# Products of zeros in the planned gaps of TensorE, in a two-layer adaLN and FFN kernel

## The chip, the cores and the metric

The kernel runs on one core of a Trainium2 chip. The metric is the device time of one execution in microseconds (us), the median of several. The engines are named as in the profile: PE (TensorE, matrix products; its weight loads are shown as PEld), DVE (VectorE), ACT (ScalarE), POOL (GpSimd) and SP (SyncE, which issues most of the DMAs).

## The reference: what is computed

`x` is 128x32x256 (batch, time, features), `cond` is 128x256. Two residual layers follow each other:

```python
# layer 0: an ODE with RK4, 32 time steps, driven by x[:, t, :], from q0 = p0 = cond
i_couple = jnp.tanh(q) @ coupling.T
dq = q - q ** 3 / 3.0 - p + drive + i_couple + bias
dp = EPSILON * (q + ALPHA - BETA * p)
...
# its trace of q goes through a gated FFN whose operands are block-quantised (blocks of 32)
inter = jax.nn.silu(_mx_linear(q, w_gate)) * _mx_linear(q, w_up)
x = x + _mx_linear(inter, w_down)
# layer 1: modulated RMS norm, attention over the 32 time steps with 16 heads of 16,
# q and k RMS-normed per head; then a gated FFN with Hadamard rotation, 8-bit activations
# and ternary weights
xn = _rms_norm(x, g_norm) * (1.0 + scale) + shift
q, k, v = split(xn @ W_qkv)
o = softmax(q @ k.T * d ** -0.5) @ v
o = o + o @ W_out
x = x + h_bitlinear(silu(h_bitlinear(o, w_gate)) * h_bitlinear(o, w_up), w_down)
```

## The kernel before

The batch of 128 fills the partitions. **Phase one** runs 32 time steps. Each step has four RK4 stages (`step`, `slope`): a PSUM slot is opened by a product of zeros (`opened`, L458), DVE adds a linear combination into it (`nest`, L513), PE adds scaled copies of the drive and of earlier stages (`plus`, L548) and the product with the coupling matrix (L562), ACT makes tanh and square (L555, L556), POOL the cube (L569). L606 makes the new state. The FFN of layer 0 for that time step (`ffn0`) follows: a transpose on PE (L487), block maxima and scales on DVE (L649, L627, L632, L639), a multiplication (L861), clipping (L841), scaling on POOL (L867, L909, L917), a DMA transpose (L395), gate and up products (L882) with silu and multiplication (L890, L894), the down product (L929). The result is stored, RMS-normed (ACT L941, POOL L946 and L947, ACT L951), multiplied and shifted on POOL (L955, L959), transposed on PE (L487) and copied to `xnT` by ACT (L964). The weights are quantised on the way: those of layer 0 in the first 90 us, mostly on DVE, the ternary ones of layer 1 near the end of the phase (PE L730, DVE L736, L740, L741, L746, L751).

**Phase two** works through 32 tiles of 128 tokens (`tokens`): q, k and v (L1043, L1050), a power on POOL for the norms (L1063, L1064), multiplication and 32x32 transposes on DVE (L1069, L1076, L1088, L1090), logits in 32x32 tiles of PE (L1098), softmax (L1113, L1117, L1120, L1121), attention times v, also in 32x32 tiles (L1128), the output rotation (L487, L1146, L1151), 8-bit quantisation (L1018, L1025, L1026, L1167, L1171), a DMA transpose, gate and up (L1184, ACT L1192, DVE L1199), a Hadamard transform (L1215 on DVE and POOL, L487, L1221, L1226), quantisation again (L1234, L1238), a DMA transpose and the down product (L1249, L1256).

**The order.** No engine takes its instructions in the order of the source. Every piece of work is an `Item` with an engine, a cost in us and the buffers that it reads and writes, and `Work` plans them. `Work.run` simulates all engines with these costs, forwards and backwards; `Work.order` repeats that up to 30 times, keeps the plan that ends first, and gives each buffer (`Buf`) its place (`Slot`). The items are then emitted in the order of their planned start, first those of phase one (rank under 100), then those of phase two, with other PSUM tiles in between. Each engine runs its instructions in that order and waits on semaphores for what it needs. The planned times are a model's: on the chip the gaps of an engine lie elsewhere or aren't there.

**PSUM slots.** A slot is a region of a PSUM bank. Slots that matter here: `ps_stage` (the RK4 stages), `ps_turn` (two halves of one bank, for transposes), `ps_gu` (two banks, gate and up of layer 0), `ps_po` (down product of layer 0); in phase two `ps_one` (four banks) and `ps_two` (two tiles of 1024 columns). A buffer takes a slot when its first writer starts, and the slot is free again when its last reader is done.

Of the kernel before, what the change touches and what calls it, by code (L numbers as in the profile page):

```python
# [20 lines left out]
P = 128  # L21
# [17 lines left out]
PE, DVE, ACT, POOL, SP = "PE", "DVE", "ACT", "POOL", "SP"  # L39
# [30 lines left out]
class Buf:  # L70


    def __init__(self, slots):
        self.slots, self.slot = slots, None
        self.writers, self.readers, self.left = [], [], 0
        self.end, self.fixed, self.pool = 0.0, False, None
# [11 lines left out]
class Item:  # L88


    def __init__(self, engine, cost, fn, rank, table, port, tail, records):
        self.engine, self.cost, self.fn, self.rank = engine, cost, fn, rank
        self.table, self.port, self.tail, self.records = table, port, tail, records
        self.after, self.before, self.open = [], [], 0
        self.bufs, self.outs, self.small, self.behind = [], (), False, ()
        self.ready, self.start, self.end = 0.0, None, None


class Work:
# [7 lines left out]
    LOAD, COLD = 1.3, 0.1  # L107
    BLOCK, FETCH = 128, 3.2
    ROUNDS = 30

    def __init__(self):
        self.items = []
# [143 lines left out]
    def order(self):  # L256

        for item in self.items:
            for a in item.after:
                a.before.append(item)  # L260
            for b in item.bufs:
                b.fixed = b.slot is not None
            item.prio = item.rank
        best = math.inf
        for n in range(self.ROUNDS):
            self.strict = n > 0
            done = self.run(True)
            end = max(item.end for item in done)
            if end < best:
                best, chosen = end, done  # L270
                places = [(b, b.slot) for item in done for b in item.bufs]
            for item in self.items:
                item.prio = -item.end
            self.strict = True
            self.run(False)
            for item in self.items:
                item.prio = -item.end
        for b, slot in places:
            b.slot = slot
        return chosen  # L280


@with_exitstack
def kernel(
# [22 lines left out]
    nc = tc.nc  # L307
    B, T, N = x.shape
# [12 lines left out]
    def tile_of(name, shape, dtype=F32):  # L321
        return const.tile(shape, dtype, name=name)
# [59 lines left out]
    work = Work()  # L382
# [69 lines left out]
    zeros = tile_of("zeros", [P, N], BF16)  # L452
# [536 lines left out]


    KPADS, VPADS = 3, 4
    PHASE_TWO = 100.0

    k_pads, v_pads = [], []
    pads_ready = []
# [35 lines left out]
    def tokens(g):  # L1031
        rank = PHASE_TWO + g
        tok = slice(g * P, (g + 1) * P)
# [228 lines left out]
        tokens(g)  # L1262

    issue = work.order()
    with tc.manual_schedule():
        for item in issue:
            if item.rank < PHASE_TWO:
                item.fn()
    phase_one.close()
    ps_2 = ctx.enter_context(tc.tile_pool(name="ps_2", bufs=1, space=PSUM))  # L1270
    for i, slot in enumerate(ps_one):
        slot.ap = ps_2.tile([P, HALF], F32, name=f"ps_one{i}")
    for i, slot in enumerate(ps_two):
        slot.ap = ps_2.tile([P, FF], F32, name=f"ps_two{i}")
    with tc.manual_schedule():
        for item in issue:
            if item.rank >= PHASE_TWO:
                item.fn()


# [50 lines left out]
```

## Time and profile before

| what | value |
|---|---|
| median of 3 runs | 874.21 us (872.87 to 882.12) |
| profiled execution | 884.23 us, its span 882.5 us |
| mean granted clock of PE | 0.956 |
| PE busy | 781.6 us (89%), 10300 products |
| PE weight loads | 590.1 us (67%) |
| DVE busy | 749.4 us (85%), 1885 instructions |
| ACT busy | 499.3 us (57%) |
| POOL busy | 636.4 us (72%) |

The span runs from the first instruction's start to the last one's end. A product's record on PE is longer than the time that it keeps the next one waiting: products are pipelined and their ends are modelled, so that "busy" holds the latency of the last one in each run. A matrix product of f32 operands appears as two records. The clock row gives the share of full speed that PE was granted. In a timeline a row is start, duration, engine, line, operation, output and inputs, shape, count, and in brackets the idle time of the engine before it, with the instruction that ended it. Phase one ends near 428 us, phase two begins with L1043 at 429.58.

### The profile page before, as it was taken

Reading aid. Unit: us, or ns where it says so; the run is one execution under the profiler, and the core shown is the slowest. Engines: PE = TensorE matmul, PEld = TensorE weight load, DVE = VectorE, ACT = ScalarE, POOL = GpSimd, SP = SyncE. Lnnn points to the kernel's source line nnn. Section 1 sums busy time; section 2 is a strip of 40 time slices with the busy share of each in tenths; the row PEclk is TensorE's granted clock in tenths of the full one; section 3 lists DMA queues with packets and bytes.
Section 4 is the critical chain, followed back from the end, with each engine's and each line's share of the span. In section 5 each row is a group of like instructions: output and inputs, shape, how many; then the busy total and the mean of one; then the engine's idle time right before and its main releaser. Section 6 shows DMA issues by size and latency. Waiting matters only on the chain. (4 is left out here: it accounts for less than half of the span.)

```text
span 882.5 us, 25579 instructions
## 1 busy us (share of the span) xinstructions
PE 781.6 (89%) x10300; PEld 590.1 (67%) x10300; DVE 749.4 (85%) x1885; ACT 499.3 (57%) x1014; POOL 636.4 (72%) x619
## 2 busy tenths in 40 slices
PE   7788999999999999994678989998999988988974
PEld 4566777778887887872344666866677665766654
DVE  5989999899999999998157978997989769798882
ACT  4243455555665665654324666767677647576653
POOL 5645898878899988799699649658866477766330
PEclk9989999999999999997769999999999989999997
DMA  8211332222322442425200122222122212122132
GB/s 265 66 32 42 71 77 57 71 57 67 70 73 73 106 99 65 105 65 99 47 2 15 24 45 48 64 56 56 19 56 56 55 36 56 37 54 44 47 70 66
DMA packets 128887, 55.49 MB, mean 63 GB/s; under 512 B 102144, under 2 KB 127616, under 8 KB 128768
## 3 DMA queue, kind: packets, MB, share of 16 engines
q1 hardware_dynamic: 128768, 53.85, 26.2%
q8 instruction: 81, 1.33, 0.6%
q14 instruction: 38, 0.31, 0.1%
HBM read 21.32 MB, written 8.39 MB: 34 GB/s over the span
## 5 line engine op out<-in xcount | busy, mean ns | idle before, releaser
L1064 POOL TENSOR_TENSOR tiny<-tiny,neg_half 128x32 f32<-128x32 f32 x32 | 175.1, 5472 | 2.7
L1215 POOL TENSOR_TENSOR wide<-wide 128x512 f32<-128x512 f32 x64 | 82.1, 1300 | 99.7 <-DVE wide L1215 60.8
L562 PEld LDWEIGHTS ps_stage<-slim,coup 128*128 128x128 f32 x1024 | 132.2, 194 | 14.3 <-ACT slim L555 5.2
L562 PE MATMUL ps_stage<-slim,coup 128*128 128x128 f32 x1024 | 138.9, 279 | 0.1
L569 POOL TENSOR_TENSOR slim<-slim,slim 128x256 f32<-128x256 f32 x96 | 73.6, 767 | 37.3 <-ACT slim L556 35.5
L1215 DVE TENSOR_TENSOR wide<-wide 128x512 f32<-128x512 f32 x128 | 87.9, 715 | 0.3
L548 PE MATMUL ps_stage<-drives,eye 128*128 128x256 f32 x256 | 81.2, 400 | 5.3 <-DVE ps_stage L513 3.8
L548 PE MATMUL ps_stage<-slim,eye 128*128 128x256 f32 x256 | 78.0, 394 | 7.6 <-DVE slim L513 7.6
L555 ACT ACTIVATE slim<-slim 128x256 f32<-128x256 f32 x96 | 39.5, 411 | 70.9 <-DVE slim L513 58.3
L1043 PE MATMUL ps_one<-w_qkv_sb,xnT 128*128 128x512 f32 x128 | 69.4, 671 | 2.1 <-DVE coup L1076 0.9
L917 POOL TENSOR_TENSOR wide_bf<-mid,tiny 128x512 bf16<-128x512 fp8e4 x64 | 67.7, 1064 | 3.9 <-DVE mid L841 3.7
L909 POOL TENSOR_TENSOR mid<-mid,tiny 128x512 f32<-128x512 f32 x64 | 66.3, 1049 | 4.1 <-DVE tiny L639 3.7
L1226 PE MATMUL ps_two<-had_ffn,wide 128*128 128x128 f32 x512 | 64.6, 282 | 4.3 <-DVE tiny L1025 1.6
L1226 PEld LDWEIGHTS ps_two<-had_ffn,wide 128*128 128x128 f32 x512 | 61.8, 196 | 8.4 <-DVE tiny L1025 2.1
L548 PEld LDWEIGHTS ps_stage<-slim,eye 128*128 128x128 f32 x256 | 43.5, 193 | 24.1 <-DVE slim L513 15.2
L1128 PEld LDWEIGHTS ps_one<-v_pad,mid 32*32 32x32 f32 x4096 | 42.2, 107 | 25.1 <-issue 15.5
L1199 DVE SCALAR_TENSOR_TENSOR wide<-ps_two,tiny,mid 128x512 f32<-128x512 f32 x64 | 46.5, 737 | 13.1 <-ACT mid L1192 12.9
L1128 PE MATMUL ps_one<-v_pad,mid 32*32 32x17 f32 x4096 | 47.8, 182 | 10.4 <-issue 5.9
L1192 ACT ACTIVATE mid<-ps_two,tiny 128x512 f32<-128x512 f32 x64 | 42.9, 686 | 21.9 <-PE ps_two L1184 21.0
L556 ACT ACTIVATE slim<-slim 128x256 f32<-128x256 f32 x96 | 38.9, 406 | 26.0 <-DVE slim L513 25.8
L1234 ACT ACTIVATE wide<-ps_two,magic,tiny 128x1024 f32<-128x1024 f32 x32 | 38.5, 1202 | 24.6 <-DVE tiny L1026 18.3
L548 PEld LDWEIGHTS ps_stage<-drives,eye 128*128 128x128 f32 x256 | 40.4, 195 | 14.3 <-DVE ps_stage L513 9.0
(153 smaller groups left out, 2065.7 us busy)
## 6 DMA issues: line engine op xcount, KB each, us to landing
x_step<-in_x_dram SPq DMA_DIRECT2D x32, 128.0 KB, 2.3
x_add<-in_x_dram SPq DMA_DIRECT2D x32, 128.0 KB, 2.1
x_dram<-slim SPq DMA_DIRECT2D x32, 128.0 KB, 1.7
slim<-x_dram SPq DMA_DIRECT2D x32, 128.0 KB, 2.2
out_dram<-slim SPq DMA_DIRECT2D x32, 128.0 KB, 1.7
raws<-in_L_ffn_w_gate_dram SPq DMA_DIRECT2D x4, 512.0 KB, 5.0
raws<-in_L_ffn_w_up_dram SPq DMA_DIRECT2D x4, 512.0 KB, 5.6
raws<-in_L_ffn_w_down_dram SPq DMA_DIRECT2D x4, 512.0 KB, 3.6
```

Of the source, the lines that this page charges most:

```text
L548: PE, cost, lambda: nc.tensor.matmul(ps[i].ap, lhsT=eyes[eye], rhs=src.ap, start=False, stop=False),
L562: nc.tensor.matmul(ps[i].ap[:, sl], lhsT=coup[i][:, c, sl], rhs=two(th.ap)[:, c, :], start=False, stop=(c == NC - 1 and m == NC - 1),)
L569: POOL, 0.685, lambda: nc.gpsimd.tensor_tensor(sq.ap, sq.ap, qi.ap, MULT),
L909: lambda it=it, ks=ks: nc.gpsimd.tensor_tensor(blocks(it.ap), blocks(it.ap), spread(binv.ap[:, ks], BLOCK), MULT),
L917: lambda b8=b8, ks=ks, sl=sl: nc.gpsimd.tensor_tensor(blocks(bq.ap[:, sl]), blocks(b8.ap), spread(bscl.ap[:, ks], BLOCK), MULT),
L1043: nc.tensor.matmul(pqk.ap, lhsT=xnT_flat[:, c, tok], rhs=w_qkv_sb[:, c, : 2 * N], start=(c == 0), stop=(c == NC - 1),)
L1064: nc.gpsimd.tensor_tensor(rstd.ap, rstd.ap, neg_half, ALU.pow)
L1128: nc.tensor.matmul(by_v(po.ap)[row, hd, :], lhsT=by_head(exT.ap)[row, hd, :], rhs=v_pad.ap[row, hd, :], start=True, stop=True,)
L1192: lambda pgu=pgu, act=act: nc.scalar.activation(act.ap, pgu.ap[:, :HALF], AF.Silu, scale=sgu.ap[:, 0:1]),
L1199: lambda pgu=pgu, act=act, sl=sl: stt(it.ap[:, sl], pgu.ap[:, HALF:], sgu.ap[:, 1:2], act.ap, MULT, MULT),
L1215: eng.tensor_tensor(dv[:, :, e, :], sv[:, :, 0, :], sv[:, :, 1, :], op)
L1226: nc.tensor.matmul(pfh.ap[:, sl], lhsT=iT.ap[:, sl], rhs=had_ffn, start=True, stop=True)
```

## The change

When the plan is made, a new method, `keep_warm`, looks through PE's items. Where the planned gap before an item is 0.45 us or more, it looks for the next PSUM buffer that waits to be opened by PE in the same phase and whose slot was last used, by the plan, before the gap begins. The item is marked with this buffer and with a count: half the planned gap divided by 0.11 us. When the item is emitted, that many products of a matrix of zeros (bf16, up to 256 columns) are emitted before it; they write to the buffer's slot, and each has a weight load of its own. The buffer's first real product writes the slot afresh. The rest of the diff stores the times of the kept plan and folds the two emitting loops into a function.

```diff
@@ class Work
+    GAP, SECOND = 0.45, 100.0
@@ order(self)
             if end < best:
                 best, chosen = end, done
                 places = [(b, b.slot) for item in done for b in item.bufs]
+                times = [(item, item.start, item.end) for item in done]
+                ends = [(b, b.end) for item in done for b in item.bufs]
@@
         for b, slot in places:
             b.slot = slot
+        for b, end in ends:
+            b.end = end
+        for item, start, end in times:
+            item.start, item.end = start, end
+        self.keep_warm(chosen)
         return chosen
+
+    def keep_warm(self, done):
+
+        pe = [item for item in done if item.engine == PE]
+        opens, last = [], {}
+        for n, item in enumerate(done):
+            for b in item.bufs:
+                if b.slots[b.slot or 0].bank:
+                    key = id(b.slots[b.slot])
+                    b_last, since = last.get(key, (None, 0.0))
+                    if b is not b_last:
+                        if item.engine == PE and b in item.outs:
+                            opens.append((item, b, since))
+                        since = 0.0
+                    last[key] = (b, max(since, b.end))
+        for prev, item in zip(pe, pe[1:]):
+            gap = item.start - prev.end
+            if gap < self.GAP:
+                continue
+            for other, b, since in opens:
+                if other.start >= item.start and since <= prev.end and (other.rank < self.SECOND) == (item.rank < self.SECOND):
+                    item.warm = (b, int(0.5 * gap / 0.11))
+                    break
@@ tile_adaln_ffn_kernel
+    def emit(second):
+
+        with tc.manual_schedule():
+            for item in issue:
+                if (item.rank >= PHASE_TWO) == second:
+                    if item.warm:
+                        b, n = item.warm
+                        cols = min(b.ap.shape[1], N)
+                        for _ in range(n):
+                            nc.tensor.matmul(b.ap[:, :cols], lhsT=zeros[:, :P], rhs=zeros[:, :cols], start=True, stop=True)
+                    item.fn()
+
+    emit(False)
     phase_one.close()
...
+    emit(True)
```

More of the change, by code (lines that the diff above doesn't have):

```diff
@@ L94, in __init__ @@
         self.after, self.before, self.open = [], [], 0
-        self.bufs, self.outs, self.small, self.behind = [], (), False, ()
+        self.bufs, self.outs, self.small, self.behind, self.warm = [], (), False, (), None
         self.ready, self.start, self.end = 0.0, None, None
@@ L991 @@
     KPADS, VPADS = 3, 4
-    PHASE_TWO = 100.0
+    PHASE_TWO = work.SECOND
     k_pads, v_pads = [], []
@@ L1264 @@
     issue = work.order()
[L1265 to L1268, printed above, removed]
+    def emit(second):
[9 more added lines that the diff above has]
+    emit(False)
     phase_one.close()
@@ L1274 @@
         slot.ap = ps_2.tile([P, FF], F32, name=f"ps_two{i}")
[L1275 to L1278, printed above, removed]
+    emit(True)
 _INS = [
```

## The prediction

> **What bounds the kernel now.** I read the page's slices first, then busy time by stage, then the same table cut finely where the clock row dips, and last the timeline around each place where the two programs' instruction orders differ.
>
> ```profile
> PE   7788999999999999994678989998999988988974
> PEclk9989999999999999997769999999999989999997
> ```
>
> PE is busy in nearly every slice but for the first two and slices 19 to 21, where the granted clock drops too. By stage (columns: length, busy time and instructions of PE, its weight loads, DVE, ACT and POOL, then granted clock, DMA share, GB/s):
>
> ```profile
> 176.00:220.00 44.00, 43.53 (x290) 34.90 (x288) 40.90 (x116) 25.38 (x73) 36.84 (x51) 1.00 0.25 59
> ...
> 400.00:420.00 20.00, 7.78 (x34) 3.99 (x33) 17.19 (x31) 6.91 (x19) 18.96 (x20) 0.71 0.52 104
> 420.00:440.00 20.00, 14.39 (x39) 7.63 (x39) 2.59 (x4) 6.27 (x15) 11.58 (x12) 0.69 0.22 44
> ...
> 550.00:600.00 50.00, 47.68 (x945) 36.55 (x943) 43.81 (x99) 36.16 (x49) 32.57 (x20) 1.00 0.28 64
> ```
>
> From 88 to 400 us PE is full (43.5 of 44) at full clock; there is no gap to fill. From 400 to 460 nothing is full: that is a chain from engine to engine, at a clock of about 0.7. From 500 on PE and DVE share the bound, at full clock almost throughout.
>
> **When the clock falls.** Cut into stretches of 3.41 us, beginning where the clock changes, the clock is constant in each:
>
> ```profile
> 43.22:46.64 3.42, 0.66 (x5) 0.32 (x3) 3.42 (x4) 0.63 (x2) 1.58 (x1) 1.00 0.13 38
> ...
> 398.21:401.62 3.41, 1.83 (x12) 0.89 (x10) 3.41 (x8) 1.96 (x6) 3.20 (x4) 1.00 0.13 29
> 401.62:405.04 3.42, 1.44 (x7) 0.68 (x8) 2.82 (x8) 1.45 (x3) 3.25 (x5) 1.00 0.95 115
> ...
> 422.10:425.52 3.42, 3.12 (x13) 1.85 (x12) 0.00 (x0) 1.01 (x5) 2.35 (x5) 0.50 0.54 102
> ...
> 428.93:432.34 3.41, 2.76 (x4) 1.21 (x5) 0.00 (x0) 0.59 (x1) 0.00 (x0) 0.50 0.02 8
> ...
> 708.82:712.24 3.42, 2.22 (x113) 1.69 (x114) 3.42 (x8) 1.58 (x4) 3.42 (x2) 1.00 0.55 43
> ```
>
> PE busy 0.66 and 1.44 us: the next stretch has half the clock. 1.83: it stays full. At half clock, 3.12 brings it back and 2.76 doesn't. 2.22 us of mostly 32x32 products (708.82) did not hold it. So I read: under about 1.6 us per stretch falls, over about 2.9 rises, small tiles count for less. The half-clock stretches add up to 77 us, but nearly all stand where PE had been waiting for somebody.
>
> **What the change adds.** The other instructions keep their order on all five engines. PE gets 259 products of 128x256 bf16, with as many weight loads, in 51 groups: 19 groups (80 products) before 96 us, 8 (56) from 376 to 430, 4 (38) from 441 to 455, 13 (34) from 461 to 830, 7 (51) from 844 to the end. Their price and the three places that matter (start, duration, engine):
>
> ```profile
> 399.13 1.05 PE L929 MATMUL ps_po<-w0dT,wide_bf 128*128 128x256 bf16 x8
> ...
> 410.99 0.59 ACT L964 COPY xnT<-ps_turn 128x256 f32<-128x256 f32 x1
> ...
> 411.63 0.40 PE L730 MATMUL ps_turn<-tiny,ones 128*128 128x1 f32 x2 [2.50 <-ACT xnT L964]
> ...
> 412.71 0.69 DVE L841 SCALAR_TENSOR_TENSOR mid<-mid,ps_sum 128x512 fp8e4<-128x512 f32 x1 [0.24 <-POOL mid L909]
> ...
> 414.57 1.89 PE L929 MATMUL ps_po<-w0dT,wide_bf 128*128 128x256 bf16 x8 [2.30 <-DMA wide_bf<-wide_bf]
> ...
> 426.94 0.60 ACT L964 COPY xnT<-ps_turn 128x256 f32<-128x256 f32 x1
> ...
> 428.47 0.44 PE L487 MATMUL ps_turn<-ident,slim 128*128 128x128 f32 x2 [1.56 <-POOL slim L959]
> ...
> 429.58 6.75 PE L1043 MATMUL ps_one<-w_qkv_sb,xnT 128*128 128x512 f32 x8 [0.68 <-ACT xnT L964]
> ...
> 435.15 5.44 POOL L1064 TENSOR_TENSOR tiny<-tiny,neg_half 128x32 f32<-128x32 f32 x1
> ```
>
> L929 has the same shape: eight cost 1.05 us at full and 1.89 at half clock, the first 0.27 and 0.42 (opened() at L458), so each further one 0.11 and 0.21 us. A group starts when PE is free and the last reader of its PSUM slot is done, not when the gap is half over; the order decides, so it runs at the head of the gap. It delays PE only by what sticks out at the end. For each group I took the start of the product before it, the end of the reader it waits for, and added n times 0.11 or 0.21. Most end well ahead of the next product.
>
> *Up to 96 us* DVE is the bound (21.9 of 22 us from 66 to 88). Ten zeros ahead of 29 us lift the stretch from 26.16 (1.29 us busy) to 2.4, so 29.57 to 32.98 keeps full clock; DVE, busy 2.96 and 3.04 us of the two stretches from 29.57, waits there at most 0.8 us for PE; I take a **gain of 0.7** (0 to 0.8). Twelve at the head of the 4.1 us gap before 48.01 lift 43.22 from 0.66 to 2.0; DVE, busy 3.14 and 2.30 us of the two half-clock stretches that follow, idles 1.4 there: **gain 0.9** (0 to 1.4). Against that, the four zeros before L458 at 40.96 wait for L861, one step later than L458 itself:
>
> ```profile
> 40.83 0.41 DVE L861 TENSOR_TENSOR slim<-ps_turn,tiny 128x256 f32<-128x256 f32 x1
> ...
> 40.96 0.27 PE L458 MATMUL ps_stage<-zeros 128*128 128x256 bf16 x1 [0.97 <-DVE states L606]
> 41.16 0.76 DVE L513 SCALAR_TENSOR_TENSOR ps_stage<-ps_sum,states 128x256 f32<-128x256 f32 x2
> ```
>
> They run from 41.29 to 41.73, L458 is 0.77 us late, and L513 on DVE, which has no idle time there, as much: **loss 0.8**. The first 12 us are at half clock either way until inputs arrive: 0.
>
> *From 400 to 460.* Eight zeros before L730 wait for the ACT copy L964, as L730 itself did (it ends at 411.58). They come wholly on top: 0.9 us at full, 1.7 at half clock. Behind L730 wait L736, L740, L741 and then L841 on DVE, with 0.24 us of slack; behind L841 the last multiplications on POOL, without a pause from 411.9 to 418.7: **loss 1.1** (0.4 to 1.4). Eighteen zeros before the transpose at 428.47 wait for L964, end 427.54: done at 429.6 at full clock (1.1 late), at 431.4 at half (3.0 late). Three more stand between the last copy, 429.53, and the first L1043: 0.3 to 0.6. In return they hold the clock at 428.93, and POOL's first L1064 needs only four of the eight L1043 records: at 0.86 each they took 3.4 us, at 0.43 they take 1.7. Net from a gain of 0.25 to, with the zeros at half clock and the clock back too late, a loss of 3.2. The full clock from 425.52 rests on 3.12 us of work in one stretch, which a shift of a few tenths undoes; so I stay near the middle: **loss 1.5**. After 435 POOL's L1064 follow one another at 5.4 us each, and PE has time. Fifteen zeros before 453.52 end at 452.8 or, at half clock, at 454.4; L1043 from 455.36 is half-clocked now, and full clock would spare 1.7 to 2.0 us: **loss 0.2** (gain 2.0 to loss 0.85).
>
> *From 461 to 830* the groups have two to four products, 34 in all. They mostly stand where the trace has no gap: 34 times 0.11 is 3.8 us of PE. Where I followed their successors, those had 0.6 to 2.4 us to spare: **loss 0.5** (0 to 3.8). The four drops of the clock in this part (480, 613, 712, 750) get hardly any zeros ahead of them.
>
> *The end.* Twenty-one zeros follow L1249 at 867.56 and end at 870.8, leaving 1.5 us in the stretch from 869.25, which is right at the limit. The last L1249 takes 1.89 us at half clock, 1.05 at full: **gain 0.4** (0 to 0.85). The six ahead of 861.44 are over by 859.1, too early for the stretch from 859.01 (0.98 busy); if it were held, L1226 would gain 1.7.
>
> **Sum.** 0.7 + 0.9 - 0.8 - 1.1 - 1.5 - 0.2 - 0.5 + 0.4 = 2.1 us slower. The profiled execution took 884.23 us (span 882.5, 1.7 around it), 10 us over the median of 874.21; 2.1 us on the median give **876.3**.
>
> [...]
>
> **Rivals.**
> 1. *The clock stays as it was*: the zeros run in the stretch before the one that decides. All gains go; losses 0.8, 1.1, 1.5 (zeros at full, products at half), 0.85, 0.5: 4.7 us, 878.9. For it: 401.62, where ten zeros end at 401.1 and change nothing. Chance 0.22.
> 2. *Zeros on the chain at half clock*, the slower side. It is decided at 427.54: if the clock is half when L964 ends, the groups that wait for a reader are paid in full: 0.8 + 1.4 + 3.2, then 0.85 at 453.52 and PE's 3.8 in the dense part: 10 us, 884.3. For it: 422.10 reached 3.12 only just. Against: the slack in the dense part. Chance 0.20.
> 3. [...] Chance 0.08.
> 4. *The clock is held everywhere*, the faster side: 0.8 + 1.4, 0.8 at L882 (404.91), 0.9 at the L929 from 423.01, 1.7 at L1043, 2.0 at 455.36, 1.7 at L1226, 0.85 at the end, less 0.8, 0.65 (eight zeros at full, slack off) and 1.5: 7.2 us, 867.0. Against it: zeros at the head of the 5.7 us gap before 422.18 leave 3.5 us idle. Chance 0.15; the time lies near the bound of 1%, and L1098 and L1128 from 447.7 to 455, at half clock too, aren't in it, so I put two thirds of the chance beyond.
>
> The forecast has 0.35. Where the stretches begin is not tied to the program, so an execution can fall either way at each limit. The three runs shown spread over 9 us, and 1% (8.7 us) is about what a measurement of this kernel can tell from no change. Faster by over 1%: 0.10 (of rival 4). Within 1%: 0.70 (the forecast, 1, 3 and the rest of 4). Slower: 0.20 (rival 2). The range, 867 to 886, reaches from rival 4 to the sum of rival 2 (10 us late) with 2 us for the spread of the runs, and leaves out the outer half of rivals 2 and 4.
>
> **What the profile will show.** Right: about 259 more records of zeros, PE's clock full from 428.9 to 432 or 18 zeros at 0.21 us there, L1064 starting 1 to 4 us later against 435.15, the same busy times from 88 to 376. Wrong, if the stretch after 429 begins earlier than before, if the zeros of the dense part show up as idle time of DVE, or if PE's gaps there shift by more than the zeros' own time.

## The result and the profile after

| what | before | after |
|---|---|---|
| median | 878.15 us (20 executions, 872.87 to 884.9) | 871.66 us (20 executions, 868.54 to 874.5) |
| ratio | 1 | **0.9926, 95% interval 0.9907 to 0.9945** |
| profiled execution | 884.23 us, span 882.5 | 872.75 us, span 870.7 |
| mean granted clock, profiled execution | 0.956 | 0.982 |
| PE busy, products | 781.6 us, 10300 | 794.3 us, 10559 |

The changed kernel is 6.5 us (0.7%) faster; the prediction was 2.1 us slower. The measured time lies inside the predicted range, on the other side of no change. The profile pair shows 11.8 us, but its first half is no typical execution: 884.2 stands 6 us over the median of its kernel, 872.75 only 1 us over. So the pair is used for places and mechanisms, and the medians for sizes.

The page of the changed kernel, slices of the span:

```profile
PE   8789999999999999996688989999998998989986
PEclk9999999999999999999699999999999999999999
```

The clock row lost its 7, 7, 6 in the middle (slices 19 to 21) but for one 6, and the 8 at the start and the 7 at the end are 9 now. The same in stages (columns as before: length, busy time and instructions of PE, weight loads, DVE, ACT, POOL, then granted clock, DMA share, GB/s):

```profile
176.00:220.00 44.00, 43.49 (x287) 34.45 (x287) 40.86 (x119) 24.78 (x70) 35.77 (x50) 1.00 0.26 64
400.00:420.00 20.00, 10.27 (x60) 6.42 (x58) 16.51 (x31) 6.67 (x19) 19.15 (x21) 0.83 0.55 108
420.00:440.00 20.00, 15.57 (x60) 9.63 (x60) 2.18 (x3) 6.19 (x15) 9.93 (x11) 0.74 0.20 40
440.00:460.00 20.00, 17.12 (x383) 12.20 (x382) 11.72 (x22) 5.71 (x10) 19.50 (x9) 0.91 0.01 2
550.00:600.00 50.00, 47.70 (x951) 37.25 (x950) 44.16 (x100) 36.00 (x48) 32.79 (x18) 1.00 0.25 58
460.00:500.00 40.00, 35.57 (x1065) 24.37 (x1065) 35.51 (x82) 20.07 (x30) 38.02 (x21) 1.00 0.14 20
```

From 400 to 440 the clock rose from 0.71 and 0.69 to 0.83 and 0.74. But that stage bought nothing: the same DVE instructions come 0.5 us earlier than before at 400 us, 0.7 us later at 450, and still 0.2 later at 470. The pair parts after that. The same DVE instructions are 2.9 us earlier at 490 to 500, 4.2 to 5.3 at 540 to 710, 7 at 740 and 7.6 at 842. The first of the large steps (3 us; the other, 3.5 us, stands at 712 to 722), in the kernel before and then in the changed one:

```profile
473.30:476.72 3.42, 2.62 (x184) 2.13 (x180) 3.02 (x10) 2.69 (x6) 3.25 (x4) 1.00 0.02 5
476.72:480.13 3.41, 1.34 (x38) 0.70 (x28) 3.31 (x7) 0.42 (x2) 3.41 (x2) 1.00 0.24 60
480.13:483.54 3.41, 3.41 (x50) 1.72 (x52) 1.76 (x4) 1.37 (x2) 2.53 (x4) 0.50 0.00 0
```

```profile
473.53:476.94 3.41, 2.55 (x122) 1.93 (x110) 3.23 (x7) 2.07 (x5) 3.24 (x4) 1.00 0.10 24
476.94:480.35 3.41, 2.75 (x58) 1.64 (x62) 3.35 (x8) 1.64 (x3) 3.41 (x2) 1.00 0.18 46
480.35:483.77 3.42, 3.42 (x129) 2.09 (x119) 3.42 (x8) 1.15 (x3) 3.42 (x4) 1.00 0.00 0
```

In the stretch from 476.7 PE is busy 1.34 us before and 2.75 after. The one is followed by half clock (a fall, from here on), and in the next stretch DVE is busy 1.76 of 3.41 us, because it waits for PE, in part by way of ACT (L1199 waits 1.53 us for ACT's L1192, which had waited 1.91 for PE's L1184, and L1113, across the stretch's end, waits 0.79 for PE's L1098); the other holds, and DVE is busy all of the next. What PE did there, before and after:

```profile
476.29 0.73 PE L1128 MATMUL ps_one<-v_pad,mid 32*32 32x17 f32 x64
478.05 0.41 PE L487 MATMUL ps_one<-ident,slim 128*128 128x128 f32 x2 [1.04 <-DVE slim L1142]
479.49 0.60 PE L1184 MATMUL ps_two<-w1gT,slim_bf 128*128 128x512 bf16 x2 [1.03 <-DMA slim_bf<-slim_bf]
```

```profile
475.74 0.49 PE L1306 MATMUL ps_one<-zeros 128*128 128x256 bf16 x3
476.16 0.73 PE L1159 MATMUL ps_one<-v_pad,mid 32*32 32x17 f32 x64
477.60 0.41 PE L518 MATMUL ps_one<-ident,slim 128*128 128x128 f32 x2 [0.71 <-DVE slim L1173]
477.84 0.59 PE L1215 MATMUL ps_two<-w1gT,slim_bf 128*128 128x512 bf16 x2
```

(The changed file's lines are 31 higher: L1215 is L1184, and so on; L1306 is the product of zeros.) The three zeros aren't even in the stretch that decides. What fills it is that L1215 doesn't wait 1.03 us for a transposing DMA as L1184 did; that transfer took 3.71 us in the kernel before's profile and 2.3 in this one. One pair of profiles can't tell a cause here from chance. The runs below go further.

### The profile page after: what moved, and what is told of

It reads as the page before. It is cut to its first block, busy times and chain, and to the rows that moved or that the text cites. A ratio compares the mean times of both kernels' runs of the same rounds, so it can differ in the third digit from the quotient of the medians.

```text
span 870.7 us, 26090 instructions
## 1 busy us (share of the span) xinstructions
PE 794.3 (91%) x10559; PEld 605.8 (70%) x10559; DVE 749.2 (86%) x1885; ACT 499.5 (57%) x1014; POOL 636.8 (73%) x619
## 3 DMA queue, kind: packets, MB, share of 16 engines
q8 instruction: 82, 1.34, 0.6%
## 5 line engine op out<-in xcount | busy, mean ns | idle before, releaser
L1095 POOL TENSOR_TENSOR tiny<-tiny,neg_half 128x32 f32<-128x32 f32 x32 | 175.1, 5473 | 2.7
L1074 PE MATMUL ps_one<-w_qkv_sb,xnT 128*128 128x512 f32 x128 | 62.7, 614 | 2.7 <-DVE coup L1107 1.9
L1257 PEld LDWEIGHTS ps_two<-had_ffn,wide 128*128 128x128 f32 x512 | 60.2, 192 | 6.5 <-issue 1.4
L1257 PE MATMUL ps_two<-had_ffn,wide 128*128 128x128 f32 x512 | 62.9, 277 | 1.7 <-DVE tiny L1056 0.9
L579 PEld LDWEIGHTS ps_stage<-slim,eye 128*128 128x128 f32 x256 | 43.0, 190 | 21.1 <-DVE slim L544 12.5
L1049 DVE TENSOR_REDUCE tiny<-ps_two 128x1 f32<-128x1024 f32 x32 | 38.8, 1213 | 12.5 <-PE ps_two L1257 10.7
```

The source lines that it names most:

```text
L579: PE, cost, lambda: nc.tensor.matmul(ps[i].ap, lhsT=eyes[eye], rhs=src.ap, start=False, stop=False),
L1049: lambda: nc.vector.tensor_reduce(am.ap[:, 0:1], src.ap[:, :n], AX.X, ALU.max, apply_absolute_value=True),
L1074: nc.tensor.matmul(pqk.ap, lhsT=xnT_flat[:, c, tok], rhs=w_qkv_sb[:, c, : 2 * N], start=(c == 0), stop=(c == NC - 1),)
L1095: nc.gpsimd.tensor_tensor(rstd.ap, rstd.ap, neg_half, ALU.pow)
L1257: nc.tensor.matmul(pfh.ap[:, sl], lhsT=iT.ap[:, sl], rhs=had_ffn, start=True, stop=True)
```

## The experiments

The 51 groups of zeros are numbered in the order in which they are emitted. Most experiments keep some groups and drop the others, with four lines at the end of `keep_warm`, where `pe` is the list of PE's items (their line numbers are 35 over those of the kernel before); only the condition differs:

```diff
+        marked = sorted((i for i in pe if i.warm), key=lambda i: i.rank >= self.SECOND)
+        for n, item in enumerate(marked):
+            if n not in range(0, 21):
+                item.warm = None
```

Each run's ratio is to executions of the kernel before on the same chip, with a 95% interval; under 1 is faster.

### Four sections, one at a time

Front (the diff above: groups 0 to 20, 84 products, up to 396 us):

> Only the 21 groups (84 products) up to 396 us are kept. Between the two profiles DVE came 1.5 us earlier by 60 us, 1.0 at 31 and 0.8 at 52, just where the half-clock stretches from 29.57 and 46.64 had stood. Theory H (the zeros hold the clock, each section for itself): 1.5 us faster, between 0.5 and 2. Rival N (the differences between two executions are where the 3.41 us stretches happen to fall, and the zeros add their own time): 0 to 1 us slower.

Middle:

```diff
+            if n not in range(21, 31):
```

> Only the 10 groups (90 products) from 402 to 455 us are kept. My prediction had a net loss of 2.8 us here; between the two profiles DVE lost 1.7 us by 435 and had it back by 480, so theory H: 0, between 1 us faster and 1 slower. Theory P (the prediction): 2.8 us slower. Rival N: 2 us slower.

Dense part:

```diff
+            if n not in range(31, 44):
```

> Only the 13 groups (34 products) from 461 to 830 us are kept. Four half-clock drops of the profile before (480, 613, 712, 750) are gone in the profile after, where one stands at 781, and DVE gained 6 us there. If the 34 zeros hold the clock (H): 3 to 6 us faster. If the drops are chance and the zeros hardly bear on them (rival N): within 1 us; prediction: 0.5 us slower.

Tail:

```diff
+            if n not in range(44, 51):
```

> Only the 7 groups (51 products) from 844 us on are kept. In the profile after, L1226 before the end and both last L1249 ran at full clock, and 4.2 us were gained from 860 on. H: 2 to 4 us faster. Prediction: 0.4 us faster. Rival N: within 0.5.

| section | products | predicted | ratio measured | mean granted clock over its executions |
|---|---|---|---|---|
| front | 84 | 0.8 us faster | 0.9997 (0.997 to 1.0025) | 0.9616 |
| middle | 90 | 2.8 us slower | 1.0013 (0.9991 to 1.0035) | 0.9686 |
| dense | 34 | 0.5 us slower | **0.994 (0.9917 to 0.9962)** | 0.9676 |
| tail | 51 | 0.4 us faster | 1.0003 (0.9976 to 1.0029) | 0.9649 |
| kernel before, same set | | | 1 (median 877.32 us) | 0.9618 |

The smallest section brings 5.3 us, and the three others nothing that can be measured. Middle and dense have nearly the same mean clock, and 877.9 against 872.7 us: how much half-clock time goes doesn't decide alone. Where it goes, and what the zeros themselves cost there, counts too; these runs don't separate the two.

### Is it the clock, and which of the 34

The same 34 products with one column in place of 256, so that their number, waits and weight loads stay and most of their time in PE goes (an estimate from the changed kernel's profile: the two f32 records of one column at 411.77, L761, start 0.03 us apart, the zeros of 256 columns 0.11 at full clock):

```diff
-                        cols = min(b.ap.shape[1], N)
+                        cols = 1
```

> The same 13 groups and 34 products as in the run with 461 to 830 us alone, with the same waits and weight loads, but each product has 1 column in place of 256. Theory H (the 256 columns keep PE active enough in the 3.41 us stretches that would fall): most of the gain goes, within 0.3% of before, with 10 us or more at half clock between 462 and 842. Rival F (68 more instructions on PE shift which ones arrive late, or the waits change the order in which PE meets its inputs): 5 us faster as with 256 columns, whatever the clock does.

Measured 0.9974 (0.9949 to 1.0): between the kernel before and the full 34, and its interval reaches 1 and overlaps that of the full 34. Its mean granted clock over twelve executions is 0.9627, against 0.9619 of the kernel before in its set; the full 34 had 0.9676 against 0.9618. But its profile has only 6.8 us at half clock between 462 and 842, where the clock theory expected 10 or more. Everything but the dense part, to see whether the rest is nothing in sum too:

```diff
+            if n in range(31, 44):
```

> The 38 other groups, 225 products, without the 13 groups from 461 to 830 us. If the sections add up: front, middle and tail gave -0.3, +1.1 and +0.3 us, together 1 us slower, within 0.3% of before. If they need each other (a shift by one section decides whether another one's zeros fall into the right stretch): 2 to 4 us faster.

Measured 0.9947 (0.9927 to 0.9968): faster by 4.7 us, though its three parts alone were at 0. This is taken up below. The dense part in two halves, the 15 products from 461 to 499 us and the 19 from 616 to 828:

```diff
+            if n not in range(31, 37):
```

> Of the 13 groups the 6 from 461 to 499 us, 15 products. Each of the four profiles without these zeros has a half-clock stretch that begins at 477 to 480, both with them have none, and DVE gained 2.4 us at 490. H: about 2 us faster and no drop at 477; the rest of the drops stays. If the drops are chance: within 1 us.

```diff
+            if n not in range(37, 44):
```

> Of the 13 groups the 7 from 616 to 828 us, 19 products. H: 3 us faster, the drop at 477 to 480 stays, those from 610 to 830 mostly go. If the gain is all at 477: within 1 us.

Early 0.9953 (0.9926 to 0.9981), late 0.999 (0.9969 to 1.0011). By these ratios the fifteen early products make most of the gain of the section. The late ones were expected to give 3 us and gave 0.9 (2.7 faster to 1 slower), and the fall expected at 477 to 480 isn't in their profile.

Then the three of them that stand just ahead of the fall at 480, alone; and the twelve others, alone:

```diff
+            if n != 33:
```

> Three products of zeros alone, the ones ahead of the first L1128 that stood at 476.29 in the kernel before. Clock theory: they lift the stretch that decides whether the clock falls at 477 to 480; the stretch at half clock there cost DVE about 1.1 us, and what follows it up to 842 us falls less often too: 2 to 4 us faster than the kernel before, no fall between 470 and 490. Rival (many small shifts of PE's instructions, each worth a little): three products do nothing, within 1 us. Rival (chance alignment: any added product among the 15 of the early dense part gives the same): also 2 to 4 us, but then the twelve others alone give as much.

```diff
+            if n not in (31, 32, 34, 35, 36):
```

> The other twelve products between 461 and 499 us, without the three before L1128. Clock theory: most of them stand on the wrong side of the stretch that decides, the fall at 477 is there, within 1.5 us of the kernel before. Rival (any added product does it): 3 to 4 us faster, as the 15 together were (0.9953).

The theory that these three do it **fell**: 1.0008 (0.9978 to 1.0038), and the clock still falls, at 477.98. The others have 0.996 (0.9934 to 0.9986), and no fall there. The stretches of the kernel with the three, from the table cut finely, and that of the kernel with the twelve:

```profile
474.57:477.98 3.41, 1.89 (x72) 1.22 (x70) 3.41 (x8) 0.74 (x2) 3.41 (x1) 1.00 0.13 27
477.98:481.39 3.41, 3.20 (x8) 1.04 (x8) 1.32 (x3) 0.69 (x1) 2.56 (x3) 0.50 0.14 38
```

```profile
475.84:479.25 3.41, 2.37 (x74) 1.39 (x73) 3.41 (x9) 0.76 (x3) 3.41 (x1) 1.00 0.25 60
```

After the stretch with 1.89 us busy, most of it 32x32 products, the clock falls, and DVE then has 1.32 busy of 3.41; with 2.37 it stays. Busy time alone doesn't draw this line: ahead of the same fall the front's profile has 2.40 us busy (118 products, from 473.63) and the middle's 2.49 (130, from 474.02), while the profile of the late products, told above, held its clock with 1.57 (8 products, none of them 32x32, from 476.45). In the profiles of all kernels that hold the twelve products (nine, in two of them with one column), the clock never falls between 476 and 481; of the eleven that don't, the kernel before among them, nine show that fall. So the twelve seem to change it, and not by standing in the stretch: in the profile of the twelve, five start at 460.84 and 465.81, and the other seven behind it, from 484.52. As one column does it too, the time of the zeros in PE isn't needed for it. What does it stays open.

All 259 products with one column:

> All 259 products with one column instead of 256: the same number of instructions, weight loads and waits at the same places, but almost no time of PE in them. Clock theory: the half-clock time goes back towards that of the kernel before (over 60 us, changed kernel 38), and the time to a ratio of 0.997 to 1.001. Rival (what counts is the number and place of the instructions, as for instance the fetching of code or the waits that order PE): the ratio stays at 0.992 to 0.994.

Measured **1.0006 (0.9977 to 1.0035)**: the whole gain is gone, with as many instructions, weight loads and waits at the same places. The mean granted clock of its twelve executions is 0.9598, against 0.9815 of the changed kernel's twenty and 0.9618 of the kernel before in its set. So the gain of the whole change needs the time that the zeros occupy PE, and it comes with the clock. A single profile doesn't separate the two as well: this kernel's profiled execution, the fastest of its twelve, has no fall at 476 to 481 either, and only one between 462 and 842, as the changed kernel. For the dense part alone (0.9974 against 0.994) the share of the clock is therefore likely, not shown.

### Clock and time over many executions

Each execution is listed with its mean granted clock, so the kernel before can be read without any change to it. Over 141 executions from the sets of this study, clock and time go together with a correlation of -0.79. The quarter with the lowest clock (mean 0.9571) took 881.7 us, that with the highest (0.9665) 875.7 us: 0.0094 of some 877 us are 8.2 us of lost clock, for 6 us of time. The program, the inputs and the order are the same; the profiles below suggest that what differs is which stretches fall. The changed kernel has a standard deviation of 1.6 us, the kernel before 2.9, and its clock ranges from 0.975 to 0.986 where the latter's goes from 0.952 to 0.971. The mean over its executions is 16.1 us of lost clock, (1 - 0.9815) times 869.8, against 33.6: 17.5 us less, for 7 us of time. At the rate within the kernel before (a fitted 0.70 us per us) it would have been 12. The clock is not worth the same everywhere: the dense part alone got back 5.3 us of lost clock for 5.3 us of time, and the run with everything but the dense part 14.3 us for 4.7.

### The groups that wait for a reader

The prediction costed four groups at 3.4 us of loss: the changed kernel without them (226 products):

```diff
+            if n in (9, 23, 25, 26):
```

> The changed kernel without the four groups that wait for a reader (four zeros at 40.96, eight at 411.63, eighteen at 428.47, three at 429.58 of the kernel before; 226 products are left). The prediction costed these at a loss of 0.8, 1.1 and 1.5: by it this kernel is 2 to 3.4 us faster than the changed one, a ratio of 0.989 to 0.990 to the kernel before. Clock theory: without the eighteen the clock is half again through the first L1074, which takes back 1 to 2 us: ratio 0.991 to 0.993.

Measured 0.9898 (0.9862 to 0.9933). Side by side with the changed kernel, in one set:

> The changed kernel once more, beside the next one. Both theories: a ratio of 0.991 to 0.994 to the kernel before.

> The changed kernel without the four groups that wait for a reader (33 of 259 products), once more. If the prediction's loss terms are real (0.8, 1.1 and 1.5 us, less what the held clock gives back): 1.5 to 3.4 us under the changed kernel of this set, a ratio lower by 0.002 to 0.004. If these groups were hidden anyway: the same as the changed kernel within 1 us.

Changed 0.9907 (0.9872 to 0.9942), median 871.68; without the four groups 0.9899 (0.9869 to 0.9928), median 871.38. The 1.5 to 3.4 us didn't come: 0.3 us, with intervals of some 3 us either way. It may be the better version, which isn't shown. The middle section without its three such groups, then with them, and the front again:

```diff
+            if n not in (21, 22, 24, 27, 28, 29, 30):
```

> The zeros between 400 and 460 us alone, without the three groups there that wait for a reader (61 of 90 products). If these groups cost what the prediction said, the middle section loses its 2.6 us of cost and keeps its gains at full clock: 1 to 3 us faster than the kernel before, a ratio of 0.9965 to 0.999 against 1.0013 with them. If they cost nothing: 1.000 to 1.002.

> The middle section alone, all 90 products, once more. If the groups that wait for a reader cost what the prediction said: 1.000 to 1.002 as before, some 3 us over the section without them (0.9968). If the earlier difference was the chip: 0.996 to 0.998.

> The front section alone, all 84 products, once more. If front and middle add, then the front is 0.997 to 0.999 here (0.9952 for both together); if they only work together, it is at 1.000 as before.

Without them 0.9968 (0.9942 to 0.9994), with them 0.999 (0.9969 to 1.0012); the medians are 877.43 and 877.42 us, and the ratios differ because the kernel before measured 880.76 us beside the one and 877.74 beside the other, on another chip. Front again: 0.9979 (0.995 to 1.0008). So these groups cost nothing that these runs show; a cost of 1 to 2 us would be within their intervals.

### Do the sections add

```diff
+            if n not in range(0, 31):
```

> The zeros of the front and the middle together (174 products). If the sections just add: 1.001, within 2 us of the kernel before. If front and middle help each other (the zeros up to 396 us and those from 402 us feed neighbouring stretches): 0.995 to 0.997.

Front and middle together: 0.9952 (0.9921 to 0.9982). Alone they have 0.9988 and 1.0002 as means of two sets each, so 0.999 if they add; all three without the dense part had 0.9947, where the product is 0.9993. They are 3 and 4 us better than their parts say, both beyond their own intervals, though the parts have such intervals too, and ran on another chip than the sums. All four, 0.9988 x 1.0002 x 1.0003 x 0.994, give 0.9933, in agreement with the 0.9926 and 0.9907 measured. Whether front and middle help each other is **not settled**.

## Why the prediction was wrong, point by point

**The step that failed** is the dense part: "They mostly stand where the trace has no gap: 34 times 0.11 is 3.8 us of PE … loss 0.5 (0 to 3.8)", with "The four drops of the clock in this part (480, 613, 712, 750) get hardly any zeros ahead of them." Measured: 5.3 us faster (3.3 to 7.3). Its bounds excluded a gain. The loss, the zeros' own time in PE, didn't show in the time, and a clock gain that the sum put at nothing is likely what came instead. The reason given is true and beside the point. The four drops are the drops of one execution. Over all profiles of kernels without the early products (at most three of the fifteen), the time from 462 to 842 us shows two to six falls, at ten different places (476 to 480, 495 to 499, 521, 596 to 597, 608 to 615, 707 to 712, 737 to 750, 780 to 784, 801 to 802, 823 to 830); in those of the six with all fifteen at full width, one or two. The two with one column have two and one as well, so that the count in single profiles doesn't prove the clock's part; the mean clocks over all their executions (0.9676 and 0.9627, above) speak for it. The falls move from kernel to kernel, and the stretches begin elsewhere from profile to profile: the prediction said so ("not tied to the program"), and drew from it that "an execution can fall either way at each limit", but gave it no price in this part. In 20 profiles the grid of stretches lies anywhere from 0.01 to 3.0 of 3.41 us against the program's start. That length is the traces' own: the clock records are 1.0 or 0.5, and all 23 changes between them in the kernel before, as all 13 in the changed one, lie whole multiples of 3.413 us apart.

**The other terms** came out wrong together, too. Front, middle and end sum to 1.6 us slower in the prediction; the one run with all of them and without the dense part was 4.7 us faster (2.8 to 6.4). One by one they were at 0, within some 2.5 us each, so which term is too dear stays open.

**The limits of the clock** that the prediction read off one profile (falls under about 1.6 us busy of 3.41, rises over about 2.9) held in kind in the changed kernel, but they are not sharp. In the changed kernel every stretch with 1.26 us busy or less was followed by half clock; 1.59 held once, and 1.61, of 57 products, didn't. Over the other profiles they overlap: the tail's held after 1.40 us busy (4 products, from 442.87), and that of the kernel without the four groups that wait for a reader fell after 1.65 (12 products, none of them 32x32, from 404.97). Of the changed kernel's stretches:

```profile
408.67:412.09 3.42, 1.19 (x11) 1.00 (x10) 1.21 (x6) 1.16 (x4) 3.34 (x5) 1.00 0.14 44
...
429.15:432.56 3.41, 2.74 (x14) 1.90 (x12) 0.00 (x0) 0.59 (x1) 0.00 (x0) 0.50 0.00 0
432.56:435.98 3.42, 3.42 (x11) 1.71 (x10) 0.58 (x1) 0.60 (x1) 0.00 (x0) 1.00 0.00 0
```

After the first the clock fell. The second, at half clock, brought it back with 2.74 us busy, where 2.76 hadn't in the kernel before: the limit of "about 2.9" isn't a sharp one. For 32x32 products 1.89 fell, as 2.22 had (2.49 us of 130 products, nearly all of them 32x32, is the most that fell), where 1.59 and 1.40 us of larger ones held: in these profiles small tiles count less, as said.

A long idle time of PE isn't needed for a fall: in the kernel before, the longest that reached into the stretch ahead of 405.04 was 2.21 us, and the fall at 480.13 followed a stretch whose longest were 1.04 and 1.03 us. Nor is the section that gained most by itself one where PE is idle for long. The kernel before's four longest idle times (5.72 us before 422.18, 4.84 before 873.43, 4.13 before 48.01, 3.79 before 447.74) are in the front, middle and tail; the dense part, where the longest from 462 to 842 us is 1.67 (before 612.6), brings 5.3 us.

**The middle** (loss 1.1, 1.5 and 0.2). The three places of the changed kernel, timeline:

```profile
410.90 1.03 PE L1306 MATMUL ps_turn<-zeros 128*128 128x256 bf16 x8 [2.93 <-ACT xnT L995]
411.77 0.28 PE L761 MATMUL ps_turn<-tiny,ones 128*128 128x1 f32 x2
...
427.33 4.00 PE L1306 MATMUL ps_turn<-zeros 128*128 128x256 bf16 x18 [0.68 <-ACT xnT L995]
431.12 0.63 PE L518 MATMUL ps_turn<-ident,slim 128*128 128x128 f32 x2
...
432.80 3.60 PE L1074 MATMUL ps_one<-w_qkv_sb,xnT 128*128 128x512 f32 x8
...
436.48 5.44 POOL L1095 TENSOR_TENSOR tiny<-tiny,neg_half 128x32 f32<-128x32 f32 x1
...
452.00 2.30 PE L1306 MATMUL ps_two<-zeros 128*128 128x256 bf16 x15
454.23 1.26 PE L1159 MATMUL ps_one<-v_pad,mid 32*32 32x17 f32 x128
455.42 1.98 PE L1074 MATMUL ps_one<-w_qkv_sb,xnT 128*128 128x512 f32 x4
```

The eight zeros start when ACT's L995 ends and stand on top for 0.87 us, as worked out. The eighteen run at half clock, 0.22 us each, and hold the transpose up until 431.12; then eight L1074 take 3.60 us at full clock where they took 6.75, and POOL's first L1095 starts at 436.48 against 435.15, 1.3 us late where 1.5 was said (1.8 by the 0.5 us that the program was ahead at 400). Without the four groups that wait for a reader it starts at 433.86, in a program that was 0.7 us further ahead at 400:

```profile
428.29 5.67 PE L1078 MATMUL ps_one<-w_qkv_sb,xnT 128*128 128x512 f32 x8 [0.68 <-ACT xnT L999]
...
433.86 5.44 POOL L1099 TENSOR_TENSOR tiny<-tiny,neg_half 128x32 f32<-128x32 f32 x1
```

What the term lacked is at 452: the upper bound of its last part ("gain 2.0") is what came. The kernel before had these:

```profile
453.52 1.91 PE L1128 MATMUL ps_one<-v_pad,mid 32*32 32x17 f32 x128 [2.15 <-DVE mid L1121]
455.36 3.78 PE L1043 MATMUL ps_one<-w_qkv_sb,xnT 128*128 128x512 f32 x4
```

With the fifteen zeros in its stretch the clock is back from 453.05, and four L1074 take 1.98 us instead of 3.78: ready at 457.40 rather than 459.14. So most of the loss ahead is given back here: the program, 0.5 us ahead at 400, is 0.2 to 0.3 us late at 460 to 470. The section alone was 1.1 us slower and 0.9 faster in its two measurements, not 2.8 slower. The mechanism was right and the sign of the last term was wrong.

**The front** (gain 0.7 and 0.9, loss 0.8). The stretch before 29.80 has 2.38 us busy, where 2.4 was said, and the clock holds from 12.7 to 46.86. The second step half came: 43.45 to 46.86 is busy 1.21 and not 2.0, so the clock fell, but for one stretch and not for two. DVE waited 0.46 us, not 0.8, for L489, which stood behind the four zeros:

```profile
40.45 0.60 PE L1306 MATMUL ps_turn<-zeros 128*128 128x256 bf16 x4 [1.30 <-DVE slim L892]
...
40.88 0.27 PE L489 MATMUL ps_stage<-zeros 128*128 128x256 bf16 x1
...
41.19 0.43 DVE L544 SCALAR_TENSOR_TENSOR ps_stage<-ps_sum,states 128x256 f32<-128x256 f32 x1 [0.46 <-PE ps_stage L489]
```

In sum 0.8 us faster predicted, 0.3 and 1.8 measured, each with some 2.5 us either way: not refuted.

**The end** (gain 0.4). Before, then after:

```profile
862.34 5.38 PE L1226 MATMUL ps_two<-had_ffn,wide 128*128 128x128 f32 x32
...
877.17 1.89 PE L1249 MATMUL ps_one<-w1dT,wide_bf 128*128 128x256 bf16 x8 [1.85 <-DMA wide_bf<-wide_bf]
```

```profile
854.70 3.91 PE L1257 MATMUL ps_two<-had_ffn,wide 128*128 128x128 f32 x32
...
859.62 2.46 PE L1306 MATMUL ps_one<-zeros 128*128 128x256 bf16 x21
864.34 1.05 PE L1280 MATMUL ps_one<-w1dT,wide_bf 128*128 128x256 bf16 x8 [2.26 <-DMA wide_bf<-wide_bf]
...
866.25 1.05 PE L1280 MATMUL ps_one<-w1dT,wide_bf 128*128 128x256 bf16 x8 [0.32 <-DMA wide_bf<-wide_bf]
```

Both steps came, the rated 0.85 and the 1.5 at L1257 that needed a held clock. The tail alone has 1.3 us at half clock in its profile, against 13.2, and measured 1.0003: their sum, 2.3 us, lies just outside its interval (2.1 faster to 2.5 slower). But the second step is partly chance: of the 14 profiles without the tail's zeros at full width, nine have that product of 32 records at 3.91 us, as the changed kernel, and five at 4.39 to 5.70; the last two L1249 are at half clock, wholly or in part, in all 14 and in none of the six others. An estimate from these profiles is 0.84 us plus a mean of 0.5, or 1.3, which the interval allows.

**The bound of 1%** as what can be told was drawn from three executions; twenty of each told 0.2%. What rival 2 said of the slower side was right about 427.54 (half clock there) and wrong that this decides. The 77 us of half clock in the prediction are 78 by the profile's records, which begin at 12.5 us.

## What to carry to other kernels

A profile shows one draw of where the clock falls (here two to six falls between 462 and 842 us in the profiles without the early products). Where the kernel runs many times, set each execution's mean clock against its time first: if they go together, as here with a correlation of -0.79, time may be had from the clock also where the profile at hand shows neither a gap nor a drop. Here 5.3 us were had where PE shares the bound with another engine (PE busy 47.7 and DVE 44.2 of 50 us from 550 on in the changed kernel); on the chain from engine to engine and in the long pauses, removing half-clock time bought nothing that could be measured section by section, and 4.7 us in the one run of all of them together.

## What was not expected of the hardware

- Two kernels with the same mean clock (0.9686 and 0.9676, same chip and set) are 5.2 us apart.
- Fifteen products that follow one another by 0.11 us, in 40 us of a span of 870, take 4.1 us off it (1.7 to 6.5); how much of that is the clock is not shown.
- The spread of a kernel's times goes with the clock (correlation -0.79): a standard deviation of 2.9 us went to 1.6 when the clock was held more.
- At half clock, a stretch busy for 2.74 us (128x256 bf16 zeros and transposes, from 429.15 in the changed kernel) brought the clock back, and one busy for 2.76 (128x512 f32 products, from 428.93 in the kernel before) didn't.
